# Counting layer 0's softmax sums once per half, with four heads in 32 columns each, and its output projection two steps later

## The chip, the cores and the metric

The kernel runs on one core of one Trainium2 chip. The metric is the device time of one execution in microseconds (us); smaller is better. Before the change the median of three executions is 3203.17 us (3202.34 to 3205.19).

## The reference

There are 16 graphs of 1024 nodes with 256 features (`x`), each with its own 0/1 adjacency matrix. Two attention layers follow each other, layer 0 with 4 heads of 64 columns, layer 1 with 8 heads of 32 columns and biases on q, k and v:

```python
h = maximum(_layernorm(x), 0)
scores = einsum('bhne,bhme->bhnm', Q, K) * scale
attn = softmax(where(adj > 0, scores, -inf), axis=-1)
heads = einsum('bhnm,bhme->bhne', attn, V)
x = x + concat(heads) @ Wo.T + bo
```

The softmax divides by a sum over all 1024 keys. The kernel leaves that division to the end: it multiplies the exponentials by V first and divides the 64 (or 32) columns of a head by the sum of its exponentials afterwards. The change is about how these sums are counted and brought to where they divide.

## The kernel before

**Tiling.** Everything is kept transposed: scores are [128 keys x 512 queries]. A *half* is 512 of a graph's 1024 queries. A *group* is the heads that fill the 128 partitions of one output tile: two heads in layer 0, four in layer 1; so a half has two groups, g = 0 and 1. A group is walked in *steps* of four score blocks of 128 x 512: four steps for a layer 0 group (two heads by two blocks of keys), eight for a layer 1 group (four heads, one block of keys). Graph b has 16 steps in layer 0 and 32 in layer 1.

**One step.** `scores` issues four matmuls (L447) into two pairs of PSUM banks. `exponentials` masks each pair on VectorE (L463, out of PSUM into the step's tile p) and exponentiates it on ScalarE (L469). Two steps later `weigh` multiplies p by V into the group's accumulator po (L481). `Stream.run` writes the order out: at an even step on which a large matmul job is due (a projection `k`, `q`, `values` or `end_half`), the weighing is put off to the next step, which then weighs two steps' tiles. So a "large" even step is followed by an odd step with a double weighing.

**Order of the steps.** After graph 0's layer 0, layer 0 of graph b+1 and layer 1 of graph b alternate. In what follows, a *period* is these 48 steps: steps 0 to 15 are layer 0 of graph b+1 (the code's `a` is step 0), steps 16 to 47 are layer 1 of graph b (the code's `c` is step 16). There are 15 periods, and 32 steps of the last layer 1 after them. `later(i, f)` hangs a job on step i; within a step, jobs stand behind the masking of that step's two pairs, large ones last.

**The buffers that matter.** All score pairs, projections and outputs share three pairs of PSUM banks (`psum_pair`, L115), taken in turn: each new pair waits until the one three before it has been read. The tile p has seven buffers for even steps and two for odd ones (L459), so the mask of an odd step waits until the odd tile of four steps before is no longer read.

**The sums before.** In layer 0, `add_tiles` (L486) adds a group's sixteen exponential blocks on VectorE (L490, L493) and GpSimd (L493, L494, L496) to one tile of [128 keys x 2 heads x 512 queries]. Four steps after the group's last weighing, `count_added` (L348) sums it over the keys on TensorE: per head one matmul with 64 columns of ones (L343), which leaves the sum in all 64 partitions of the head in the PSUM tile pz. In layer 1 GpSimd adds the odd step's tile to the even step's (L582, 128 x 2048 elements) and DMAs with addition (L568) join two such sums; TensorE counts four heads of 32 columns in one go.

Then the chain of a group: `spread` copies pz to the tile s on ScalarE (L362) and spreads one row per head over the partitions by DMA (L375); `invert` takes the reciprocal on VectorE (L383) and writes it to DRAM (L385); `fetch` reads it back broadcast to the head's partitions, into the tile inv (L393); `normalize` multiplies the group's half of `cat` by it on GpSimd (L399); `end_half` multiplies `cat` by Wo (L429, 16 records on TensorE) and adds the result to x (L434). `end_group` (L611) sets their steps. For layer 0 they come 4, 6, 7, 9 and 11 steps after the group's last weighing. In a period the four groups of layer 0 are counted at steps 9, 13, 17 and 21, normalized at steps 14, 18, 22 and 26, and the two halves are projected at steps 20 and 28. `block_inputs(mine, 1, ...)` at L766 puts the q projection of layer 1's second half on step 22.

s and inv have one buffer each. The reciprocals' DRAM tiles have four buffers for each layer.

Of the kernel before, what the change touches and what calls it, by code (L numbers as in the profile page):

```python
# [10 lines left out]
F32 = mybir.dt.float32  # L11
# [7 lines left out]
P = 128  # L19
# [69 lines left out]
def fast_program(ctx, tc, a, w, loads, chk):  # L89
# [3 lines left out]
    nc = tc.nc  # L93
    x, adj, out = a["x"], a["adj"], a["out"]
    B, N, E = x.shape
# [216 lines left out]
    class Group:  # L312


        def __init__(self, inp, mask, qh, g, half):
            self.inp, self.mask, self.qh, self.g, self.half = inp, mask, qh, g, half
            self.layer = inp.layer
            self.D = E // HEADS[self.layer]
            self.per = P // self.D
            self.scale = 1.0 / math.sqrt(self.D)  # L320
            self.n = f"{inp.n}_{qh}_{g}"
            self.n_f = self.per * 512 // P
            self.last = qh == QH - 1 and g == 1

            self.hurry = False

            self.waits = ((6, 6), (7, 7), (8, 6), None)[2 * qh + g]

            self.brief, self.pairs = self.last and inp.b == B - 2, False
# [8 lines left out]
        def count(self, p, start, stop):  # L338

            if start:  # L340
                self.s = ps_o.tile([P, 512], F32, tag="pz", name=f"pz_{self.n}")
            for r in range(self.per):
                nc.tensor.matmul(  # L343
                    self.s[r * self.D : (r + 1) * self.D, :], w.ones.to_broadcast([P, self.D]), p[:, r, :],
                    start=start, stop=stop,
                )

        def count_added(self):  # L348
            self.count(self.t, True, True)

        def copy_out(self):
            if self.g == 0:
# [5 lines left out]

        def spread(self):

            s = work.tile([P, 512], F32, tag="s", bufs=1, name=f"s_{self.n}")
            nc.scalar.copy(tiled(s), by_tile(self.s))  # L362
            inp, k = self.inp, 2 * self.qh + self.g
            if k == 0:

                pool, tag = small, f"sums{self.layer}"
                if self.layer and inp.b == B - 1:
                    pool, tag = adjp, "adj"
                inp.sums = pool.tile(
                    [P, 4 * self.n_f], F32, tag=tag, bufs=1, name=f"sums_{inp.n}"  # L370
                )
            self.sn = inp.sums[:, ts(k, self.n_f)]
            lanes = P // self.per
            for r in range(self.per):
                nc.sync.dma_start(  # L375
                    self.sn[r * lanes : (r + 1) * lanes, :],
                    s[r * self.D : r * self.D + 1, :].rearrange("r (c f) -> r c f", f=self.n_f),
                )

        def invert(self):  # L380

            vn = small.tile([P, self.n_f], F32, tag="vn", bufs=1, name=f"vn_{self.n}")
            nc.vector.reciprocal(vn, self.sn)  # L383
            vd = dram.tile([self.per, 512], F32, tag=f"vd{self.layer}", name=f"vd_{self.n}")
            nc.sync.dma_start(self.lanes(vd), vn)  # L385
            self.vd = vd

        def fetch(self):

            vd = self.vd  # L390
            self.inv = work.tile([P, 512], F32, tag="inv", bufs=1, name=f"inv_{self.n}")
            for r in range(self.per):
                nc.sync.dma_start(  # L393
                    self.inv[r * self.D : (r + 1) * self.D, :], vd[r].partition_broadcast(self.D)
                )

        def normalize(self):
            o = self.half.cat[:, self.g, :]
            nc.gpsimd.tensor_mul(o, o, self.inv)  # L399

        def finish(self):

            inp, qh = self.inp, self.qh
            inv = work.tile([P, 512], F32, tag="inv", bufs=1, name=f"inv_{self.n}")
            py = psum_pair(f"py_{self.n}").rearrange("p a (t e) -> p (a t) e", e=E)
            rows, cat = xs[inp.b, qh], self.half.cat
            dst = quarters(out, inp.b, qh)
            for h in range(2):
                q = ts(h, 256)
                nc.vector.reciprocal(tiled(inv)[:, ts(h, 2)], by_tile(self.s)[:, ts(h, 2)])  # L410
                nc.vector.tensor_mul(cat[:, self.g, q], cat[:, self.g, q], inv[:, q])
                for i in (2 * h, 2 * h + 1):
                    for c in range(2):
                        nc.tensor.matmul(
                            py[:, i, :], cat[:, c, ts(i, P)], w.o[self.layer][:, c, :],
                            start=(c == 0), stop=(c == 1),
                        )
            for h in range(2):
                t = ts(h, 2)
                nc.vector.tensor_add(rows[:, t, :], py[:, t, :], rows[:, t, :])  # L420
                for g in range(4):
                    nc.sync.dma_start(dst[g][:, t, :], rows[ts(g, 32), t, :])
# [84 lines left out]
    class Stream:  # L507
# [103 lines left out]
        def end_group(self, i, gr):  # L611

            if gr.hurry:
                for f in (gr.spread, gr.finish, gr.inp.test):
                    self.later(i, f)
                return

            if gr.layer == 0:
                self.later(i + 4, gr.count_added)
                at = 4, 6, 7, 9, 11  # L620
            else:
                at = ((6, 12, 15, 19), (7, 12, 14, 17, 19), (6, 9, 11, 14), None)[2 * gr.qh + gr.g]
                if gr.pairs:
                    at = 2, 5, 6, 7, 9
                elif gr.last:
                    at = 4, 6, 7, 9, 11
            for k, f in zip(at, (gr.spread, gr.invert, gr.fetch, gr.normalize)):
                self.later(i + k, f)
            if gr.last:

                k = 7 if gr.layer or gr.inp.b == 0 else 37
                self.later(i + k if gr.inp.b + gr.layer < B - 1 else len(self.steps) + 2, gr.inp.test)
            if gr.g == 1:
                self.later(i + at[4], gr.end_half)
# [119 lines left out]
    for b in range(B - 1):  # L754
        mine, a, c = inputs[1][b], first[b + 1], second[b]
        if b == 0:

            norms(mine, 0, a + 5, a + 6, a + 8, a + 9, whole=True)
            half_inputs(mine, 0, a + 11, a + 12, a + 14, a + 14)
            norms(mine, 1, a + 13, a + 14, a + 15, c, whole=True)  # L760
            half_inputs(mine, 1, c + 1, c + 3, c + 6, c + 4)
        else:
            norms(mine, 0, a - 20, a - 16, a - 15, a - 14, bias=a)
            block_inputs(mine, 0, a - 10, a - 8, a - 4, a, a + 2, a + 8)
            norms(mine, 1, a - 14, a - 10, a - 8, a - 6, bias=a + 6)
            block_inputs(mine, 1, a, a + 6, a + 7, c, c + 6, c + 2)  # L766
        for i, u in zip((0, 2, 4, 6, 8, 10, 12, 13), range(NT)):
            later(a + i, masks[b].second, u)
        if b + 2 < B:
# [275 lines left out]
```

## Time and profile before

| what | before |
|---|---|
| median of three executions | 3203.17 us |
| the profiled execution, its own time | 3201.31 us |
| its span, first to last instruction | 3199.5 us |
| granted TensorE clock, mean | 0.997 |
| VectorE busy | 2532.5 us, 79% |
| GpSimd busy | 2352.4 us, 74% |
| ScalarE busy | 2242.4 us, 70% |
| layer 0's counting matmuls (L343, 64 columns), 256 records | 66.5 us |
| layer 1's counting matmuls (L343, 32 columns), 992 records | 129.5 us |
| copies of pz (L362), 128 | 72.9 us |
| normalizing multiplications (L399), 127 | 185.4 us |
| layer 0's reciprocals (L383, 128 x 8), 64 | 12.0 us |

One fp32 matmul leaves two records in the profile, so layer 0's 256 records are 128 matmuls, two for each of 64 groups. Matmuls on disjoint columns of the array run beside each other, so the time of such a set is read from the start of the first to the start of what follows.

From the start of one step's scores to the next, the profile shows the same pattern in every period from the second on; a period takes between 195.1 and 195.6 us. These are step lengths of the sixth period (layer 0 of graph 6, layer 1 of graph 5), whose step 0 starts 1113.76 us into the span:

| step | 9 | 13 | 17 | 20 | 21 | 22 | 26 | 27 | 28 | 29 | 30 | 31 |
|---|---|---|---|---|---|---|---|---|---|---|---|---|
| us | 6.36 | 6.36 | 5.51 | 4.72 | 3.93 | 4.70 | 2.15 | 3.21 | 4.75 | 2.92 | 2.07 | 3.29 |

The profile's engines are PE (TensorE's matmuls), PEld (its weight loads), DVE (VectorE), ACT (ScalarE), POOL (GpSimd) and SP (the queue that issues most DMAs).

### The profile page before, as it was taken

To read this page: it belongs to the slowest core of one execution; us is meant where nothing else is said; L and a number is where in the kernel's file an instruction comes from. 1 tells how busy PE (TensorE), PEld (TensorE's weight loads), DVE (VectorE), ACT (ScalarE), POOL (GpSimd) and SP (SyncE) were. 2 spreads that over 40 slices of the span, in tenths; PEclk is the share of its full clock that TensorE was granted. 3 is DMA by queue.
4 is the path that set the end of the run, shared out by engine and by line. 5 is a ranking of instruction groups with operands and counts; after the bars stand their busy time and mean duration, and the time that the engine had idled before them with its cause. 6 is when DMAs were issued, how large, how long until landed. Compare 5 with 4: busy or idle time off the path is not lost.

```text
span 3199.5 us, 44432 instructions
## 1 busy us (share of the span) xinstructions
PE 3153.7 (99%) x16662; PEld 1212.4 (38%) x16662; DVE 2532.5 (79%) x2786; ACT 2242.4 (70%) x2472; POOL 2352.4 (74%) x1103
## 2 busy tenths in 40 slices
PE   8999999999999999999999999999999999999998
PEld 3443433433334333333433334343343333333332
DVE  5677787887878888787887878878788887887776
ACT  5667677776767767677676776767777676775765
POOL 4567677786877868678686776877778687786776
PEclk9999999999999999999999999999999999999999
DMA  6326556364563645646465463655636456462321
GB/s 132 53 47 131 108 112 130 88 135 106 111 134 92 130 104 109 131 99 129 95 127 117 101 134 92 131 104 112 135 88 133 108 111 135 91 131 62 85 62 32
DMA packets 347792, 341.21 MB, mean 107 GB/s; under 512 B 196016, under 2 KB 290480, under 8 KB 330544
## 3 DMA queue, kind: packets, MB, share of 16 engines
q0 software_dynamic: 37584, 173.03, 29.2%
q1 hardware_dynamic: 309984, 165.26, 21.5%
q8 instruction: 133, 2.18, 0.3%
q14 instruction: 91, 0.75, 0.1%
HBM read 149.95 MB, written 47.96 MB: 62 GB/s over the span
## 4 chain that ended last, share of the span: by engine, by line
PE 89%; ACT 4%; DVE 3%; POOL 2%; issue 1%; DMA 1%; SPq 0%; DVEq 0%; POOLq 0%; ACTq 0%
PE ps L447 31%; PE po L481 27%; PE pq L266 13%; PE py L429 7%; PE pv L302 6%; PE pz L343 5%; DVE p L463 2%; ACT p L469 2%; ACT hn L210 1%; ACT mask L163 1%; POOL p L582 1%; POOL rstd L199 0%; ACT v L306 0%; DVE st L191 0%; DMA hT<-turned 0%
## 5 line engine op out<-in xcount | busy, mean ns | idle before, releaser
L463 DVE SCALAR_TENSOR_TENSOR p<-mask,ps 128x1024 f32<-128x1024 fp8e5 x1536 | 1796.8, 1212 | 461.3 <-PE ps L447 423.6
L469 ACT ACTIVATE p<-p 128x1024 f32<-128x1024 f32 x1536 | 1609.4, 1056 | 784.9 <-DVE p L463 745.4
L582 POOL TENSOR_TENSOR p<-p,p 128x2048 f32<-128x2048 f32 x255 | 1171.3, 4596 | 250.0 <-PE po L481 152.3
L447 PE MATMUL ps<-qT,kT 32*128 32x512 f32 (+1 forms) x6144 | 1134.1, 631 | 7.2 <-ACT v L306 4.4
L481 PE MATMUL po<-p,v 128*32 128x512 f32 (+1 forms) x6144 | 990.6, 601 | 2.1 <-ACT cat L354 1.8
L447 PEld LDWEIGHTS ps<-qT,kT 32*128 32x128 f32 (+1 forms) x6144 | 363.7, 184 | 706.2 <-issue 308.6
L494 POOL TENSOR_TENSOR p<-p 128x1024 f32<-128x1024 f32 x128 | 301.9, 2358 | 284.0 <-DVE p L493 275.3
L481 PEld LDWEIGHTS po<-p,v 128*32 128x32 f32 (+1 forms) x6144 | 229.2, 118 | 690.8 <-issue 500.3
L493 POOL TENSOR_TENSOR p<-p 128x1024 f32<-128x1024 f32 x64 | 150.8, 2357 | 173.3 <-DVE p L490 101.5
L266 PE MATMUL pq<-hT,wk 128*128 128x512 f32 x512 | 242.8, 618 | 8.9 <-DMA hT<-turned 6.3
L302 PE MATMUL pv<-wv,hT 128*128 128x256 f32 x1024 | 237.8, 385 | 0.0
L266 PE MATMUL pq<-hT,wq 128*128 128x512 f32 x512 | 236.6, 605 | 0.0
L429 PE MATMUL py<-wo,cat 128*128 128x256 f32 x1008 | 235.5, 386 | 0.5 <-POOL cat L399 0.2
L302 PEld LDWEIGHTS pv<-wv,hT 128*128 128x128 f32 x1024 | 189.4, 190 | 70.5 <-DVE p L463 30.4
L429 PEld LDWEIGHTS py<-wo,cat 128*128 128x128 f32 x1008 | 185.6, 190 | 72.5 <-issue 31.4
L343 PE MATMUL pz<-p,ones 128*32 128x512 f32 (+1 forms) x1248 | 196.1, 595 | 0.8 <-ACT s L362 0.8
L399 POOL TENSOR_TENSOR cat<-cat,inv 128x512 f32<-128x512 f32 x127 | 185.4, 1460 | 5.0 <-DMA inv<-vd 3.1
L219 POOL TENSOR_TENSOR x<-x,bo 128x1024 f32<-128x1024 f32 x64 | 152.1, 2376 | 15.8 <-DMA bo<-in_bo_dram 15.8
L490 DVE TENSOR_TENSOR p<-p 128x1024 f32<-128x1024 f32 x128 | 163.2, 1275 | 0.0
L210 ACT ACTIVATE hn<-x,shift,rstd 128x256 f32<-128x256 f32 x256 | 138.2, 588 | 24.9 <-DMA turned<-hn 17.7
L496 POOL TENSOR_TENSOR p<-p,p 128x1024 f32<-128x1024 f32 x64 | 151.5, 2367 | 5.0
L266 PEld LDWEIGHTS pq<-hT,wk 128*128 128x128 f32 x512 | 94.4, 194 | 153.3 <-issue 112.9
(51 smaller groups left out, 1665.4 us busy)
## 6 DMA issues: line engine op xcount, KB each, us to landing
p<-p POOLq DMA_DIRECT2D x133, 1024.0 KB, 7.7
adj<-in_adj_dram POOLq DMA_DIRECT2D x128, 256.0 KB, 4.2
turned<-hn SPq DMA_DIRECT2D x58, 512.0 KB, 2.9
hT<-turned SPq DMA_DIRECT2D x232, 128.0 KB, 3.1
x<-in_x_dram SPq DMA_DIRECT2D x128, 128.0 KB, 2.7
inv<-vd SPq DMA_DIRECT2D x128, 128.0 KB, 2.9
inv<-vd SPq DMA_DIRECT2D x252, 64.0 KB, 3.6
out_dram<-x SPq DMA_DIRECT2D x124, 128.0 KB, 2.4
```

Source lines behind the costliest of these rows:

```text
L210: nc.scalar.activation(hn[:, ts(i, E)] if whole else self.blocks(half)[:, :, i, :], rows if whole else rows.rearrange("p (c q) -> p c q", ...
L266: nc.tensor.matmul(pq[:, m, :], wt[self.layer][:, c, ts(m, P)], self.hT[half][:, c, :], start=(c == 0), stop=(c == 1),)
L302: nc.tensor.matmul(pv[:, i, :], self.hT[half][:, c, ts(i, P)], w.v[self.layer][:, c, :], start=(c == 0), stop=(c == 1),)
L343: nc.tensor.matmul(self.s[r * self.D : (r + 1) * self.D, :], w.ones.to_broadcast([P, self.D]), p[:, r, :], start=start, stop=stop,)
L399: nc.gpsimd.tensor_mul(o, o, self.inv)
L429: nc.tensor.matmul(py[:, i, :], self.half.cat[:, c, ts(i, P)], w.o[self.layer][:, c, :], start=(c == 0), stop=(c == 1),)
L447: nc.tensor.matmul(st.ps[i // 2][:, i % 2, :], gr.inp.kT[r * D : (r + 1) * D, gr.g, ts(kt, P)], gr.inp.qT[gr.qh][r * D : (r + 1) * D, gr.g ...
L463: nc.vector.scalar_tensor_tensor(out=half, in0=gr.mask.m[gr.qh][:, kt, :].unsqueeze(1).to_broadcast([P, 2, 512]), scalar=-EDGE if gr.layer ...
L469: nc.scalar.activation(half, half, AF.Exp, scale=gr.scale)
L481: nc.tensor.matmul(gr.o[r * D : (r + 1) * D, :], gr.inp.v[:, kt, h * D : (h + 1) * D], st.p[:, i, :], start=(kt == 0), stop=(kt == NT - 1),)
L494: nc.gpsimd.tensor_add(a, a, b)
L582: nc.gpsimd.tensor_add(one, one, st.p)
```

## The change

Layer 0's sums are counted once for a half. When the first group (g = 0) ends, nothing is scheduled but its summed tile is remembered. At the second group's count, four matmuls with 32 columns of ones each count all four heads, side by side. So there is one copy out of pz, one spread (now four DMAs of one row to 32 partitions), one reciprocal (128 x 16 in place of two of 128 x 8) and one write to DRAM for a half. `fetch` reads two tiles inv, one for each group, and `normalize` does both multiplications one behind the other at the step at which the second group's stood.

s and inv now come from one ring of two buffers (the tag "inv" of the pool `work`), and both layers' reciprocals from one ring of four DRAM tiles.

For graphs 1 to 14 layer 0's `end_half` stands 13 steps behind the last weighing in place of 11: in a period the projections move from steps 20 and 28 to 22 and 30. The q projection of layer 1's second half moves from step 22 to 20 (for periods with the block inputs and graphs below the last). Graph 0's and graph 15's projections stay where they were.

```diff
-            self.n_f = self.per * 512 // P
+            self.n_f = 16
...
-            for r in range(self.per):
+            for r, of in enumerate(p if type(p) is list else [p[:, r, :] for r in range(4)]):
                 nc.tensor.matmul(
-                    self.s[r * self.D : (r + 1) * self.D, :], w.ones.to_broadcast([P, self.D]), p[:, r, :],
-                    start=start, stop=stop,
+                    self.s[ts(r, 32), :], w.ones.to_broadcast([P, 32]), of, start=start, stop=stop
                 )
 
         def count_added(self):
-            self.count(self.t, True, True)
+            both = self.half.first.t, self.t
+            self.count([t[:, r, :] for t in both for r in range(2)], True, True)
...
-            s = work.tile([P, 512], F32, tag="s", bufs=1, name=f"s_{self.n}")
+            s = work.tile([P, 512], F32, tag="inv", name=f"s_{self.n}")
...
-            inp, k = self.inp, 2 * self.qh + self.g
+            inp, k = self.inp, 2 * self.qh + self.g if self.layer else self.qh
...
-            lanes = P // self.per
-            for r in range(self.per):
+            for r in range(4):
                 nc.sync.dma_start(
-                    self.sn[r * lanes : (r + 1) * lanes, :],
-                    s[r * self.D : r * self.D + 1, :].rearrange("r (c f) -> r c f", f=self.n_f),
+                    self.sn[ts(r, 32), :],
+                    s[32 * r : 32 * r + 1, :].rearrange("r (c f) -> r c f", f=self.n_f),
                 )
...
-            vd = dram.tile([self.per, 512], F32, tag=f"vd{self.layer}", name=f"vd_{self.n}")
+            vd = dram.tile([4, 512], F32, tag="vd", name=f"vd_{self.n}")
...
-            self.inv = work.tile([P, 512], F32, tag="inv", bufs=1, name=f"inv_{self.n}")
-            for r in range(self.per):
-                nc.sync.dma_start(
-                    self.inv[r * self.D : (r + 1) * self.D, :], vd[r].partition_broadcast(self.D)
-                )
+            self.inv = {}
+            for g in (self.g,) if self.layer else range(2):
+                inv = self.inv[g] = work.tile([P, 512], F32, tag="inv", name=f"inv_{self.n}_{g}")
+                for r in range(self.per):
+                    nc.sync.dma_start(
+                        inv[ts(r, self.D), :],
+                        self.vd[r if self.layer else 2 * g + r].partition_broadcast(self.D),
+                    )
 
         def normalize(self):
-            o = self.half.cat[:, self.g, :]
-            nc.gpsimd.tensor_mul(o, o, self.inv)
+            for g, inv in self.inv.items():
+                o = self.half.cat[:, g, :]
+                nc.gpsimd.tensor_mul(o, o, inv)
...
             if gr.layer == 0:
+                if gr.g == 0:
+                    gr.half.first = gr
+                    return
                 self.later(i + 4, gr.count_added)
-                at = 4, 6, 7, 9, 11
+                at = 4, 6, 7, 9, 13 if 0 < gr.inp.b < B - 1 else 11
...
-            block_inputs(mine, 1, a, a + 6, a + 7, c, c + 6, c + 2)
+            block_inputs(mine, 1, a, a + 6, a + 7, c, c + (4 if b < B - 2 else 6), c + 2)
```

## The prediction

> **What bounds the kernel now.** I read the busy shares and the chain of waits first, then the sums by stage of one period, then TensorE's timeline, last the other engines' around the moved projection.
>
> ```profile
> PE 3153.7 (99%) x16662; PEld 1212.4 (38%) x16662; DVE 2532.5 (79%) x2786; ACT 2242.4 (70%) x2472; POOL 2352.4 (74%) x1103
> PE 89%; ACT 4%; DVE 3%; POOL 2%; issue 1%; DMA 1%; SPq 0%; DVEq 0%; POOLq 0%; ACTq 0%
> ```
>
> TensorE is busy nearly always and carries most of the chain. A busy matmul may still be one that waits inside, so I go by starts. The sixth period's two stages (layer 0, then layer 1; columns: window, length, then busy time and instructions of each engine):
>
> ```profile
> core 0: us, PE busy (x) PEld busy (x) DVE busy (x) ACT busy (x) POOL busy (x), PEclk, DMA share, GB/s
> 1113.76:1192.89 79.13, 79.13 (x341) 30.97 (x337) 63.99 (x64) 51.06 (x56) 53.28 (x28) 1.00 0.48 106
> 1192.89:1308.90 116.01, 115.67 (x698) 44.01 (x696) 95.05 (x111) 88.17 (x99) 94.45 (x42) 1.00 0.59 119
> ```
>
> In layer 0 the others have slack: VectorE 64 of 79 us, GpSimd 53. In layer 1 VectorE and GpSimd stand at 95 and 94 of 116: little slack, and only as long as TensorE's large jobs, which need neither, are spread evenly.
>
> **What the counting gives.** TensorE's timeline in layer 0 (start, time, instruction); steps 5 and 9 each count one set, the first four heads in 32 columns (layer 1's), the second two in 64:
>
> ```profile
> 1141.62 3.65 PE L481 MATMUL po<-p,v 128*64 128x512 f32 x16
> 1145.20 1.06 PE L343 MATMUL pz<-p,ones 128*32 128x512 f32 x8
> 1146.19 1.99 PE L447 MATMUL ps<-qT,kT 64*128 64x512 f32 x8
> ...
> 1161.25 3.65 PE L481 MATMUL po<-p,v 128*64 128x512 f32 x16
> 1164.73 1.03 PE L343 MATMUL pz<-p,ones 128*64 128x512 f32 x4
> 1165.69 1.99 PE L447 MATMUL ps<-qT,kT 64*128 64x512 f32 x8
> ```
>
> From start to start a set of two takes 1165.69 - 1164.73 = 0.96 us, a set of four 0.99: they do run side by side. But the weighing ahead takes 1145.20 - 1141.62 = 3.58 before the set of four and 3.48 before the set of two. So among 64-column work a set of four costs 0.99 + 0.10 - 0.96 = 0.13 more.
>
> Step 9 and step 17 lose a set (0.96 each, of 64 columns among 64-column work). Step 13 exchanges its set: 0.13 more. Step 21 stands among layer 1's 32-column work, where sets of four take 0.97 (1253.05 - 1252.08 below in the same view): even. That is 1.92 - 0.13 = 1.79 us less TensorE work in each period.
>
> The Trainium skill, "TensorEngine Tiling (Array Packing)", section "Tiling Modes", says that changing the tiling mode drains the array. It speaks against the change at step 13 alone and gives no figure; the 0.13 agrees with it. Left out, it would make the gain 1.92 a period, 2 us more in all.
>
> What else goes (a ScalarE copy of 72.9/128 = 0.57, a reciprocal of 0.19, DMAs) lies beside TensorE's work and is worth nothing here.
>
> **What the move costs.** The end of the second half, steps 25 to 31. Steps start at 1231.73, 1234.66, 1236.81, 1240.02 (28), 1244.77, 1247.69, 1249.76 (31), 1253.05 (32).
>
> ```profile
> 1234.05 4.57 POOL L582 TENSOR_TENSOR p<-p,p 128x2048 f32<-128x2048 f32 x1 [3.07 <-PE po L481]
> 1238.65 2.35 DVE L463 SCALAR_TENSOR_TENSOR p<-mask,ps 128x1024 f32<-128x1024 fp8e5 x2 [0.47 <-POOL p L582]
> 1238.92 0.89 POOL L568 DMA_DIRECT2D p<-p  x1 [0.30 <-POOL p L582]
> 1239.53 1.59 POOL L399 TENSOR_TENSOR cat<-cat,inv 128x512 f32<-128x512 f32 x1
> 1240.78 4.84 POOL L582 TENSOR_TENSOR p<-p,p 128x2048 f32<-128x2048 f32 x1
> 1241.15 3.69 PE L429 MATMUL py<-wo,cat 128*128 128x256 f32 x16
> 1241.19 2.35 DVE L463 SCALAR_TENSOR_TENSOR p<-mask,ps 128x1024 f32<-128x1024 fp8e5 x2 [0.19 <-PE ps L447]
> 1248.87 2.35 DVE L463 SCALAR_TENSOR_TENSOR p<-mask,ps 128x1024 f32<-128x1024 fp8e5 x2 [0.50 <-PE ps L447]
> 1249.76 1.51 PE L447 MATMUL ps<-qT,kT 32*128 32x512 f32 x8
> ```
>
> Two rules are seen. An odd step's mask waits for GpSimd's add of the odd tile four steps before (only two odd buffers): step 27's starts at 1238.65, 0.03 behind the add that ends at 1238.62. And the second pair of scores waits for a free PSUM pair: step 31's scores wait for the first mask of step 30, which ends at 1248.87 + 1.21 = 1250.08, and the weighing follows 1.12 later (1251.20).
>
> Now the projection leaves step 28, and GpSimd gets a second normalization ahead of the add at 1240.78. In the old clock, with steps up to 27 as they are:
>
> - Step 28: scores 1.07, weighing 1.00 (step 30's: 1249.76 - 1248.76). Ends 1242.09 in place of 1244.77. Its masks stay at 1241.19 to 1243.54, then four statistics until 1244.78.
> - Step 29: its second scores wait for step 28's first mask (1242.40); the weighing starts at 1243.51, the step ends at 1244.51.
> - GpSimd: the add ends at 1245.62 before; a normalization more (1.29, its median) makes it 1246.91. Step 29's masks start at 1246.94; the first ends at 1248.15, the second at 1249.29.
> - Step 30: from 1244.51 its second scores wait until 1248.15, so end at 1249.26. The projection, in the pair that step 29's second mask frees, runs from 1249.3 for 3.62. Ends 1252.92.
> - Step 31: scores 1.07, the double weighing 1.85, the count 0.97. Ends 1256.8, against 1253.05: **3.8 us later**.
>
> The projection's own time is only moved; TensorE stands idle in step 30 for 1249.26 - 1244.51 - 1.07 = 3.7 us. The large jobs at 24 and 30 now leave five small steps between them, in which GpSimd needs 4.57 for every two and TensorE only 4.1. Large jobs at 32 and 34 let everything catch up, so I expect nothing further. Bounds: if the added normalization cost nothing, the add ends at 1245.62 and the loss is 2.5; if GpSimd held nobody, the mask would follow the statistics at 1244.78, and 1.6 is lost still. Upward, a normalization of 1.59, as in the row: 4.1. I take 3.8, because step 27's and 31's masks start right at the add's end.
>
> **The other steps.** The spread is four DMAs in place of two. Before layer 1, VectorE waits for them:
>
> ```profile
> 1191.53 1.28 SPq L375 DMA_DIRECT2D sums<-s  x2
> 1194.18 0.20 DVE L383 RECIPROCAL vn<-sums 128x8 f32<-128x8 f32 x1 [0.41 <-DMA sums<-s]
> ```
>
> Two more issues of 0.64 delay this reciprocal by 1.28, and behind it the masks of steps 16 and 17, their sums and the kernel's whole VectorE queue. TensorE's large jobs in 16 and 18 hide most: step 18's masks come behind step 17's two adds, and step 19's second scores would wait about 0.5. Bounds 0 and 1.28; I take 0.3.
>
> At step 18 two normalizations stand ahead of the first layer 1 add: it ends about 1.3 later, and step 21's mask by up to 1; step 22's scores have that much room, so 0. The projection and the q projection change places between 20 and 22; both take some 3.65 of TensorE. The second half's two fetches are issued until 1231.71 now; two more of 0.59 each and the 3.1 to landing make it about 1236, before the normalization at 1239.53. The ring of s and inv: each allocation finds its buffer's normalization or spread past, since s and inv alternate in layer 1; 0. The first group's summed tile is held until step 13 or 21 and its buffer wanted at 16 or 24; 0.
>
> **The sum.** Graphs 1 to 14: 14 x (3.8 + 0.3 - 1.79) = 32.3. Graph 0 keeps its place: -1.79 at most, but it lies in the first period with other waits; -0.9. Graph 15 keeps the projection two steps behind two normalizations: -1.79 and up to 1.29 twice; -0.3. Together +31 on the profiled execution's 3201.3 (span 3199.5, 1.8 around it), that is 3232; the median stands 1.9 above it: **3234 us**.
>
> **The rivals.**
>
> - *Faster: the wait stays covered.* If step 29's mask isn't held (the adds run earlier than I reckon), only counting changes: 15 x 1.79 + 0.9 = 28 less, 3175. For it: TensorE 99% busy, and all such waits on the add come to little now:
>
> ```profile
> DVE p L463 <- POOL p L582: 35.4, 62, 1.2
> ```
>
>   Against: 62 waits show that the adds already end last at odd steps; only the projection at 28 covers step 29's. Chance 0.1.
> - *About no change.* The loss at the lower bound 1.6 to 2.0: 14 x (1.8 - 1.79) - 1.2, so 3202. Needs GpSimd's order not to matter. Chance 0.07.
> - *Slower still: the reciprocal's wait reaches TensorE in full.* 14 x (1.28 - 0.3) = 14 more, 3248. Against: VectorE idles 0.60 before step 18's masks and 2.37 before step 19's (its timeline), which takes up 1.28. Chance 0.1.
> - *Slower, smaller: the loss is near 2.5* because the two normalizations overlap the add: 14 x (2.5 + 0.3 - 1.79) - 1.2 = 13, so 3216. Chance 0.15.
>
> My forecast has the rest, 0.58, with 3225 to 3243 for it. The range takes in the two other slower cases and stops short of no change: 3207 to 3250. No change is within 0.2%, 6.4 us, which is about what measurements here can tell. Faster 0.10, same 0.07, slower 0.83.
>
> **What would show it.** Step 13 0.13 longer, 9 and 17 0.96 shorter. Step 30 some 8.4 us long, with VectorE's masks of step 29 released by the add L582, starting some 4.8 us behind step 29's start; waits of masks on L582 up from 35 to about 80 us. If step 30 takes 4.7, my reading of the odd buffers is wrong, and the kernel is faster. If the loss appears at step 19 too, the spread's DMAs are dearer than I took them.

## The result, and the profile after

| | before | after |
|---|---|---|
| median, us | 3203.28 (3202.34 to 3205.19, 4 runs) | 3310.12 (3309.36 to 3313.82, 4 runs) |
| ratio after/before, 95% interval | | 1.0335 [1.0317, 1.0353] |
| profiled execution, its span, us | 3201.3, 3199.5 | 3310.66, 3308.8 |
| granted TensorE clock, mean | 0.997 | 0.987 |

The kernel is 107 us slower. The forecast was 3234, +31: the direction held, the size was missed by a factor of three, and the time lies 60 us outside the range. In the kernel after, the lines named here stand three further down: L447 is L450, L463 L466, L469 L472, L481 L484, L582 L585, L568 L571, L399 L402, L429 L432.

The busy shares of the profile after, and its chain of work by engine:

```profile
PE 3209.7 (97%) x16662; PEld 1232.4 (37%) x16662; DVE 2568.8 (78%) x2754; ACT 2220.1 (67%) x2440; POOL 2348.8 (71%) x1103
PE 69%; DVE 9%; POOL 9%; ACT 5%; issue 3%; DMA 3%; SPq 1%; ACTq 0%; DVEq 0%; POOLq 0%
```

TensorE has as many records as before (16662), is busy 56 us longer, and yet carries only 69% of the chain in place of 89%. VectorE and GpSimd hold 9% each now, where they held 3% and 2%. The same two stages as before, in the sixth period (window, length, then the engines' busy times, granted clock, DMA share, GB/s):

```profile
core 0: us, PE busy (x) PEld busy (x) DVE busy (x) ACT busy (x) POOL busy (x), PEclk, DMA share, GB/s
1146.05:1225.30 79.25, 78.55 (x340) 30.54 (x337) 64.70 (x63) 50.48 (x55) 52.01 (x27) 1.00 0.46 102
1225.30:1350.98 125.68, 122.44 (x699) 46.47 (x697) 97.14 (x110) 87.42 (x99) 95.71 (x43) 0.97 0.54 113
```

Layer 0 keeps its length (79.25 for 79.13), layer 1 takes 9.7 us more at a clock of 0.97 in place of 1.00. Taken apart by step, from the start of one step's scores to the next, as a mean over the third to the fourteenth period (after less before, us):

| step | 9 | 12 | 13 | 17 | 21 | 22 | 24 | 25 | 28 | 29 | 30 | 31 | period |
|---|---|---|---|---|---|---|---|---|---|---|---|---|---|
| us | -0.86 | +0.84 | +0.14 | -0.67 | -0.04 | +1.27 | +0.68 | +1.25 | -2.68 | -0.49 | +8.73 | +0.49 | +8.66 |

The periods sum to 108 of the span's 109. So there are four losses: at step 30, at 22, at 24 and 25, and at 12.

**Step 30.** The timeline of the end of the second half, after (start, time, instruction; in brackets the idle time ahead and what ended it; here and below, rows of other instructions between these are left out). Step 29 starts at 1277.51, step 30 at 1279.95, step 31 at 1291.24:

```profile
1276.19 1.58 POOL L402 TENSOR_TENSOR cat<-cat,inv 128x512 f32<-128x512 f32 x1
1277.44 4.82 POOL L585 TENSOR_TENSOR p<-p,p 128x2048 f32<-128x2048 f32 x1
1279.95 1.13 PE L450 MATMUL ps<-qT,kT 32*128 32x512 f32 x4
1282.29 4.62 DVE L466 SCALAR_TENSOR_TENSOR p<-mask,ps 128x1024 f32<-128x1024 fp8e5 x4 [2.09 <-POOL p L585]
1283.57 2.08 PE L450 MATMUL ps<-qT,kT 32*128 32x512 f32 x4 [2.49 <-DVE p L466]
1285.57 5.74 PE L432 MATMUL py<-wo,cat 128*128 128x256 f32 x16
```

The odd buffer's wait is there as drawn: add, mask (1282.29, 4.78 behind step 29's start), then the second scores. But these scores then take 2.08 for 1.13, and the projection 5.74 for the 3.7 of before. The windows view of the same place says why:

```profile
1282.87:1289.69 6.82, 6.12 (x14) 3.81 (x15) 4.04 (x4) 4.23 (x4) 5.35 (x2) 0.50 0.57 96
```

For 6.82 us TensorE was granted half its clock. This is a second cost behind the wait, which the prediction doesn't have.

**Step 22.** It should start its second scores at once. The timeline there:

```profile
1246.16 4.53 POOL L585 TENSOR_TENSOR p<-p,p 128x2048 f32<-128x2048 f32 x1
1248.33 2.39 DVE L195 TENSOR_TENSOR ve<-mv,numbers 128x4 f32<-128x4 f32 x1
1250.72 1.40 DVE L278 TENSOR_SCALAR qT<-pq,bq 128x512 f32<-128x512 f32 x2
1252.04 1.20 DVE L466 SCALAR_TENSOR_TENSOR p<-mask,ps 128x1024 f32<-128x1024 fp8e5 x1
1252.17 1.13 PE L450 MATMUL ps<-qT,kT 32*128 32x512 f32 x4
```

Before, the sixth period's rows at that place were these (step 20 starts at 1210.75, step 21 at 1215.47, step 22 at 1219.40):

```profile
1210.33 4.55 POOL L582 TENSOR_TENSOR p<-p,p 128x2048 f32<-128x2048 f32 x1
1215.54 0.16 DVE L195 TENSOR_TENSOR ve<-mv,numbers 128x4 f32<-128x4 f32 x1
```

L195 adds eps to four variances per partition. Before, it took 0.16 us there; now 2.39, and it ends at 1250.72, 0.03 behind the end of GpSimd's add (1246.16 + 4.53 = 1250.69). VectorE's queue stands behind it, step 21's mask with it, and step 22's second scores wait for that mask. The Trainium skill, "SBUF — State Buffer", section "SBUF: two separate sides", has the reason: VectorE and GpSimd share a pair of ports under an exclusive lock, and a VectorE operation with two SBUF inputs blocks for the whole of a GpSimd operation that reads SBUF. The trace agrees: mv and eps both lie in SBUF, and the end times meet within 0.03 us; L191 and L192 just ahead, with one input in SBUF, run inside the same add in their usual 0.42 and 0.18 us.

The add gets into L195's way because it is late: as a mean of the twelve periods it starts 2.58 us behind step 20's start, where before it started 0.18 ahead of it. Of these 2.76 us the second normalization makes 1.2. The other 1.5 stand ahead of it: GpSimd's last adds of layer 0 wait for an add of VectorE, and that comes later (1.11 behind step 18's start in place of 0.42 ahead), for the greater part because VectorE waits longer for the first half's reciprocal: 1.50 us a period in place of 0.63.

**Steps 24 and 25.** The timeline around the second half's spread:

```profile
1256.92 0.94 POOL L571 DMA_DIRECT2D p<-p  x1 [0.30 <-POOL p L585]
1256.94 3.34 SPq L375 DMA_DIRECT2D sums<-s  x4
1261.65 1.24 DVE L236 STREAM_TRANSPOSE hn<-hn 128x1024 f32<-128x1024 f32 x1
1264.66 0.25 DVE L383 RECIPROCAL vn<-sums 128x16 f32<-128x16 f32 x1 [1.77 <-DMA sums<-s]
1264.83 2.28 DVE L466 SCALAR_TENSOR_TENSOR p<-mask,ps 128x1024 f32<-128x1024 fp8e5 x2
```

The four small transfers are issued just behind GpSimd's adding DMA of a whole tile, and land late. The issue-to-landing times of the tile s there:

```profile
DMA to landing us min/median/max: 1.7/5.8/6.2
```

Before, GpSimd's adding DMA came behind the two spreads, and both landed within 1.8 us:

```profile
1221.74 1.13 SPq L375 DMA_DIRECT2D sums<-s  x2
1222.64 0.94 POOL L568 DMA_DIRECT2D p<-p  x1 [0.30 <-POOL p L582]
```

The reciprocal is on time in VectorE's queue and waits 1.77 us, with the masks behind it. Over the twelve periods the second half's spreads take 5.9 us to landing as a median, in place of 1.7, and the reciprocal waits 2.17 as a mean, in place of nothing.

**Step 12** gives back what step 9 won:

```profile
1203.39 2.36 POOL L219 TENSOR_TENSOR x<-x,bo 128x1024 f32<-128x1024 f32 x1
1205.71 2.25 POOL L402 TENSOR_TENSOR cat<-cat,inv 128x512 f32<-128x512 f32 x1
1206.61 0.70 PE L432 MATMUL py<-wo,cat 128*128 128x256 f32 x2
1208.01 3.29 PE L432 MATMUL py<-wo,cat 128*128 128x256 f32 x14 [0.70 <-POOL cat L402]
```

TensorE comes 0.86 us earlier to layer 1's projection. GpSimd's bias addition L219 and the normalization behind it are no earlier (counted from step 9's start, the normalization begins at 14.09 now and at 14.11 before), and the projection waits for them.

Two lines of the waits after (total, times, longest), where before had 35.4 and 7.5:

```profile
DVE p L466 <- POOL p L585: 56.1, 61, 2.1
DVE vn L383 <- DMA sums<-s: 46.7, 26, 3.0
```

### The profile page after: what moved, and what is told of

Its sections match the earlier page's. It is cut to its first block, busy times and chain, and to the rows that moved or that the text cites. A ratio compares the mean times of both kernels' runs of the same rounds, so it can differ in the third digit from the quotient of the medians.

```text
span 3308.8 us, 44304 instructions
## 1 busy us (share of the span) xinstructions
PE 3209.7 (97%) x16662; PEld 1232.4 (37%) x16662; DVE 2568.8 (78%) x2754; ACT 2220.1 (67%) x2440; POOL 2348.8 (71%) x1103
## 4 chain that ended last, share of the span: by engine, by line
PE 69%; DVE 9%; POOL 9%; ACT 5%; issue 3%; DMA 3%; SPq 1%; ACTq 0%; DVEq 0%; POOLq 0%
PE ps L450 24%; PE po L484 21%; PE pq L266 10%; PE py L432 6%; DVE p L466 5%; PE pv L302 5%; POOL p L585 4%; PE pz L343 3%; POOL cat L402 2%; ACT p L472 2%; DMA sums<-s 2%; ACT hn L210 1%; SPq L375 1%; POOL p L497 1%; POOL x L219 1%
## 5 line engine op out<-in xcount | busy, mean ns | idle before, releaser
L472 ACT ACTIVATE p<-p 128x1024 f32<-128x1024 f32 x1536 | 1607.5, 1056 | 926.5 <-DVE p L466 892.8
L466 DVE SCALAR_TENSOR_TENSOR p<-mask,ps 128x1024 f32<-128x1024 fp8e5 x1536 | 1794.5, 1213 | 435.4 <-PE ps L450 377.5
L585 POOL TENSOR_TENSOR p<-p,p 128x2048 f32<-128x2048 f32 x255 | 1169.6, 4589 | 324.1 <-PE po L484 225.7
L450 PE MATMUL ps<-qT,kT 32*128 32x512 f32 (+1 forms) x6144 | 1189.8, 634 | 50.6 <-DVE p L466 43.1
L484 PE MATMUL po<-p,v 128*32 128x512 f32 (+1 forms) x6144 | 992.1, 602 | 2.4 <-ACT cat L354 2.4
L450 PEld LDWEIGHTS ps<-qT,kT 32*128 32x128 f32 (+1 forms) x6144 | 377.5, 184 | 788.2 <-issue 305.1
L484 PEld LDWEIGHTS po<-p,v 128*32 128x32 f32 (+1 forms) x6144 | 229.3, 118 | 690.9 <-issue 490.1
L432 PE MATMUL py<-wo,cat 128*128 128x256 f32 x1008 | 261.6, 415 | 12.0 <-POOL cat L402 10.4
L432 PEld LDWEIGHTS py<-wo,cat 128*128 128x128 f32 x1008 | 203.0, 207 | 99.8 <-issue 49.3
L402 POOL TENSOR_TENSOR cat<-cat,inv 128x512 f32<-128x512 f32 x127 | 178.3, 1448 | 5.5 <-DMA inv<-vd 3.4
L437 DVE TENSOR_TENSOR x<-py,x 128x1024 f32<-128x1024 f32 x63 | 77.0, 1222 | 127.7 <-PE py L432 127.7
L493 DVE TENSOR_TENSOR p<-p 128x1024 f32<-128x1024 f32 x128 | 173.7, 1357 | 0.0
L219 POOL TENSOR_TENSOR x<-x,bo 128x1024 f32<-128x1024 f32 x64 | 152.7, 2387 | 16.0 <-DMA bo<-in_bo_dram 15.6
L343 PE MATMUL pz<-p,ones 128*32 128x512 f32 x1248 | 163.2, 595 | 0.8 <-ACT s L362 0.8
```

The lines of the kernel that those rows point to most:

```text
L219: nc.gpsimd.tensor_add(rows, rows, w.bo[self.layer].unsqueeze(1).to_broadcast([P, 4, E]))
L343: nc.tensor.matmul(self.s[ts(r, 32), :], w.ones.to_broadcast([P, 32]), of, start=start, stop=stop)
L402: nc.gpsimd.tensor_mul(o, o, inv)
L432: nc.tensor.matmul(py[:, i, :], self.half.cat[:, c, ts(i, P)], w.o[self.layer][:, c, :], start=(c == 0), stop=(c == 1),)
L450: nc.tensor.matmul(st.ps[i // 2][:, i % 2, :], gr.inp.kT[r * D : (r + 1) * D, gr.g, ts(kt, P)], gr.inp.qT[gr.qh][r * D : (r + 1) * D, gr.g ...
L466: nc.vector.scalar_tensor_tensor(out=half, in0=gr.mask.m[gr.qh][:, kt, :].unsqueeze(1).to_broadcast([P, 2, 512]), scalar=-EDGE if gr.layer ...
```

## The experiments

Each kernel's time is compared with the kernel before on the same chip (medians 3200.8 for e1 to e4, 3202.9 for e5 to e8, 3201.5 for e9 to e12). Step changes are means over the same twelve periods. e1 to e6 and e9 were executed once each, the others four to ten times.

**e1: the two moves alone**, on the kernel before.

```diff
-                at = 4, 6, 7, 9, 11
+                at = 4, 6, 7, 9, 13 if 0 < gr.inp.b < B - 1 else 11
-            block_inputs(mine, 1, a, a + 6, a + 7, c, c + 6, c + 2)
+            block_inputs(mine, 1, a, a + 6, a + 7, c, c + (4 if b < B - 2 else 6), c + 2)
```

> The kernel before with only the steps moved (projections of layer 0 at 22 and 30, q at 20); counting as before, one normalization ahead of each add. If the odd buffers are what stalls step 30 (the add of steps 24 and 25 ends when it did, at 1245.62 of the old clock, and no projection covers step 29's mask), step 30 loses about 2.5 us a period and the kernel takes about 3238; if TensorE's clock halves behind that wait as it does in the changed kernel, up to 2.8 more a period, about 3275. If the second normalization is what stalls it, nothing is lost here and the time stays within 10 us of 3203. Steps 22, 24 and 25 stay as before in either case.

Measured: 3243.27. Only steps 28 to 31 change: -2.68, -0.49, +5.70, +0.49. In nine of the twelve periods the four come to +2.4 to 2.6; in the rest to 4.0 or 5.7. Step 30 in the sixth and in the ninth period, by windows:

```profile
1258.31:1265.58 7.27, 5.87 (x28) 3.55 (x25) 4.84 (x6) 4.34 (x5) 6.97 (x4) 1.00 0.52 88
1852.16:1862.59 10.43, 9.17 (x28) 5.45 (x24) 4.84 (x6) 4.34 (x5) 7.05 (x4) 0.67 0.61 114
```

The other engines' work is the same in both to 0.1 us; the clock is 1.00 in one and 0.67 in the other, and 3.16 us lie between. So the odd buffer's wait costs 2.5 a period without the second normalization, and the clock up to 3.2 on top, in some periods.

**e2: the counting alone**, both moves undone in the kernel after.

```diff
-                at = 4, 6, 7, 9, 13 if 0 < gr.inp.b < B - 1 else 11
+                at = 4, 6, 7, 9, 11
-            block_inputs(mine, 1, a, a + 6, a + 7, c, c + (4 if b < B - 2 else 6), c + 2)
+            block_inputs(mine, 1, a, a + 6, a + 7, c, c + 6, c + 2)
```

> The changed kernel with the projections back at 20 and 28 and q at 22; the sums still counted once. If the move makes the loss at steps 28 to 31 (6 us a period), it goes, but the projection at 28 waits up to 1.3 for the second normalization, and the losses of steps 12, 22, 24 and 25 (0.9, 1.3, 0.6, 1.1) stay: 3203 + 14 x (0.86 - 0.86 - 0.86 + 0.14 + 3.0 + 1.3) = about 3250, no half clock. If all losses came from the move, only the counting's gain is left: 3175 to 3195.

Measured: 3237.85. The counting by itself is 37 us slower, where the prediction gave its matmuls a gain of 28 and took off 4 for the first half's reciprocal. Steps 9, 12, 13, 24 and 25 change as in the kernel after; 22 does not (the q projection is back in it), but 20 loses 1.15 and 28 0.76, both steps with a projection. The projection waits there for the second normalization; step 28 of the sixth period:

```profile
1253.88 0.70 PE L432 MATMUL py<-wo,cat 128*128 128x256 f32 x2
1255.11 3.29 PE L432 MATMUL py<-wo,cat 128*128 128x256 f32 x14 [0.53 <-POOL cat L402]
```

At step 20 it waits 0.37 for the first and 0.52 for the second. The clock stays at 0.997. e1's +42 and e2's +37 come to 80, not 107: the second normalization and the move meet in steps 28 to 31, which lose 6.05 together and 3.02 and 0.76 apart.

**e3: layer 0's first normalization on VectorE**, so that the add behind the pair is not later.

```diff
-                nc.gpsimd.tensor_mul(o, o, inv)
+                (nc.gpsimd if g or self.layer else nc.vector).tensor_mul(o, o, inv)
```

> The changed kernel with the first group's normalization on VectorE in place of GpSimd, so that one stands ahead of each add as before. If the second normalization costs what it delays the adds by, step 29's mask starts 1.3 earlier, step 30 is 1.3 shorter (up to 4 if the clock no longer halves), and step 22's 1.3 goes: 3310 - 14 x 2.6 = about 3274, down to 3235 without half clocks. If the second normalization is hidden and only the move counts, within 10 us of 3310.

Measured: 3276.83. Step 22 loses 0.33 in place of 1.27, steps 28 to 31 together 3.9 in place of 6.05; 24 and 25 stay at +2.07. So the second normalization on GpSimd accounts for most of step 22's loss and for some 2 us of that at steps 28 to 31. What is left there lies near e1's 3.02, where one normalization stands ahead of the add too.

**e4: the two small statistics operations on GpSimd**, L195 and L197, in the kernel after.

```diff
-                nc.vector.tensor_add(ve, mv[:, :, 1], w.eps)
+                nc.gpsimd.tensor_add(ve, mv[:, :, 1], w.eps)
-                nc.vector.tensor_mul(less, mv[:, :, 0], w.minus)
+                nc.gpsimd.tensor_mul(less, mv[:, :, 0], w.minus)
```

> The changed kernel with the two 128 x 4 operations of the layer norm's statistics (lines 195 and 197) on GpSimd, where the power that reads them runs anyway. If step 22's loss of 1.27 us is VectorE held at line 195 by GpSimd's add (2.39 us in place of 0.16), step 22 goes back to 4.7 and the kernel to about 3310 - 14 x 1.27 = 3292. If step 22 loses by the q projection's two copies standing where one add to x stood, it stays, and the time with it (within 6 us).

Measured: 3267.25, some 25 us better than expected. Step 22's loss is gone, and all that left VectorE's queue are the two small operations. Not all of it need be the port at this one place, for the add starts earlier too, 1.79 behind step 20's start in place of 2.58. But in e5, below, it starts at 1.70 with L195 still on VectorE, and step 22 loses 0.49. Steps 24 and 25 fall from +1.93 to +0.41 as well: with step 22 on time, the spread is issued ahead of L571, and three of its four transfers land in 1.7 us. Steps 28 to 31 stay at +6.12. In the sixth period, where the clock happens to hold, step 30 reads:

```profile
1259.51:1267.99 8.48, 5.88 (x29) 3.56 (x25) 4.83 (x6) 4.35 (x5) 8.18 (x4) 1.00 0.40 71
```

8.48 us at full clock, where the prediction wrote "some 8.4 us"; in periods at half clock it takes 9.6 to 11.7.

**e5: the reciprocal one step later** for layer 0, and the fetch with it.

```diff
-                at = 4, 6, 7, 9, 13 if 0 < gr.inp.b < B - 1 else 11
+                at = 4, 7, 8, 9, 13 if 0 < gr.inp.b < B - 1 else 11
```

> The changed kernel with invert and fetch of layer 0 one step later (7 and 8 in place of 6 and 7). If steps 24 and 25 lose 1.9 us a period because VectorE stands at the reciprocal waiting for the four spreading DMAs, that goes: 3310 - 14 x 1.9 = about 3284. If they lose it because all of VectorE is late from step 22 on (line 195), most of it stays and the time is within 10 us of 3310.

Measured: 3278.57. Steps 24 and 25 lose nothing now, so the reciprocal's wait was their cause. Step 22's loss falls to 0.49, which I hadn't expected. The trace gives the reason: the first half's reciprocal no longer waits either, VectorE's add behind it comes 0.9 earlier, GpSimd's adds with it, and L195 is held for 1.46 us in place of 2.39. The second half's spreads still take 5.9 us to landing (median), but nobody waits for them: the reciprocal's wait there falls from 2.17 to 0.16. Steps 28 to 31 lose 6.58, with TensorE at half clock for 6.8 us in 13 of the 15 periods.

**e6: layer 1's bias addition one step later**, on e2.

```diff
-                norms(other, 1, c, c + 4, c + 5, c + 6, bias=c + 42)
+                norms(other, 1, c, c + 4, c + 5, c + 6, bias=c + 43)
```

> The changed kernel with the projections back (as e2, 3238), and GpSimd's addition of the bias to x (line 219, 2.4 us) one step later, so that it stands behind layer 1's last normalization of a period and not ahead of it. If step 12 gives back what step 9 saved because the projection there waits for that normalization, step 12's 0.84 goes: 3238 - 12 = about 3226. If step 12 is slower for another cause (the tiling mode, the weights), it stays at 3238.

Measured: 3217.74. Step 12 goes from +0.84 to -0.16: the bias ahead of the normalization in GpSimd's queue was what it waited for. Step 20's loss falls from 1.15 to 0.45. Steps 24, 25 and 28 remain.

**e7: all the mendings at once**: the counting without the moves, counted and brought one or two steps earlier, with e4's and e6's edits.

```diff
-                self.later(i + 4, gr.count_added)
-                at = 4, 6, 7, 9, 13 if 0 < gr.inp.b < B - 1 else 11
+                self.later(i + 3, gr.count_added)
+                at = 3, 5, 6, 7, 11
```

> The sums counted once for a half as in the change, but one step earlier (count and spread 3 steps behind the last weighing, invert 5, fetch 6, both normalizations 7, where GpSimd waits for TensorE anyway; projections back at 11, q at 22), the statistics' two small operations on GpSimd and the bias one step later. If the counting is worth what the steps 9, 13, 17 and 21 show (about 1.75 us a period) and all losses were collisions of its chain with GpSimd's adds, VectorE's queue and the projections, this takes 3203 - 28 = about 3175. If two normalizations and four DMAs cost by themselves wherever they stand, it stays above 3203.

Measured: 3212.35, ratio 1.0032 [1.0019, 1.0044]: a miss by 37 us. Steps 22, 24 and 25 are clean; step 28 loses 2.02 and step 19 0.94 (the +0.84 at step 12 and +1.00 at step 20 are counting sets moved there). The second half's `fetch` now meets the adding DMA that `spread` met before (L571 is issued at 1223.37, the first fetch at 1224.31). Timeline:

```profile
1232.61 2.53 POOL L402 TENSOR_TENSOR cat<-cat,inv 128x512 f32<-128x512 f32 x2 [1.94 <-DMA inv<-vd]
1235.10 4.58 POOL L585 TENSOR_TENSOR p<-p,p 128x2048 f32<-128x2048 f32 x1
1239.71 4.61 DVE L466 SCALAR_TENSOR_TENSOR p<-mask,ps 128x1024 f32<-128x1024 fp8e5 x4 [1.83 <-POOL p L585]
```

The landing times of the tile inv there:

```profile
DMA to landing us min/median/max: 5.8/7.2/7.8
```

A late fetch holds the normalizations, they hold the add, the add holds an odd mask: the odd buffer's wait once more, set off by a transfer.

**e8: e4's and e6's edits on the kernel before**, to see what they are worth without the counting.

> The kernel before with only the two side edits of e7: the statistics' two small operations on GpSimd and the bias one step later. The time per step of the kernel before has no stall at steps 12 or 20 to 25, so I expect 3190 to 3205; a clear gain here would have to be taken off the gain of e7.

Measured: 3197.16, ratio 0.9982 [0.9973, 0.9992]. By steps: -0.16 at step 12, -1.35 in graph 0's layer 0, little else.

**e9: three odd buffers and six even ones**, in the kernel after.

```diff
-        st.p = pp.tile([P, 4, 512], F32, tag=f"p{odd}", bufs=2 if odd else 7, name=f"p_{st.n}")
+        st.p = pp.tile([P, 4, 512], F32, tag=f"p{odd}", bufs=3 if odd else 6, name=f"p_{st.n}")
```

(The two tiles of these tags that stage the first adjacencies follow.)

> The changed kernel with three buffers for the tiles of odd steps and six for those of even steps (two and seven before). If step 29's mask waits at GpSimd's add because there are two odd buffers, it now starts behind the statistics, step 30's wait falls below what halves TensorE's clock (about 0.6 to 1.6 us left in place of 3.8), and no half clock follows: step 30 loses 1 to 2 instead of 8.7 a period and the kernel takes 3310 - 14 x 7 = about 3215. If step 30 waits for something else, it stays at 3310.

Measured: 3249.72. Steps 28 to 31 lose 1.53 in place of 6.05. Step 30 in the sixth period, by windows, and step 29's masks in the timeline:

```profile
1259.60:1265.87 6.27, 5.87 (x28) 3.55 (x24) 4.83 (x6) 4.35 (x5) 6.27 (x3) 1.00 0.39 65
```

```profile
1257.09 4.83 POOL L585 TENSOR_TENSOR p<-p,p 128x2048 f32<-128x2048 f32 x1
1259.77 2.33 DVE L466 SCALAR_TENSOR_TENSOR p<-mask,ps 128x1024 f32<-128x1024 fp8e5 x2
1262.19 4.83 POOL L585 TENSOR_TENSOR p<-p,p 128x2048 f32<-128x2048 f32 x1
```

The masks start in the middle of the add and wait for nothing, and step 30 keeps the full clock. The 4.5 us that go are the odd buffer's wait and what the clock made of it. The time is 35 us above what I expected, because steps 12, 22, 24 and 25 stay at +0.84, +1.24, +0.64 and +1.46: I had put too much of the whole on step 30.

**e10: three odd buffers in the kernel before.**

> The kernel before with the same buffers. It waits for the odd buffers 35 us in 62 places, nearly all covered: 3195 to 3203; more than 3210 if six even buffers are too few.

Measured: 3198.48, ratio 0.9991 [0.9982, 1.0001]: about nothing, since before no odd wait reaches TensorE.

**e11: e7 with the reciprocal and the fetch one step earlier still**, and layer 1's other bias addition later.

```diff
-                at = 3, 5, 6, 7, 11
+                at = 3, 4, 5, 7, 11
-                norms(other, 0, a + 10, a + 12, a + 13, a + 15)
+                norms(other, 0, a + 10, a + 12, a + 13, a + 15, bias=c + 36)
```

> As e7, with invert and fetch one step earlier again (4 and 5), so that the reciprocals' DMAs are issued ahead of GpSimd's 1 MB adding DMA of step 22 and not behind it, and GpSimd's bias addition of layer 0's first half out of the way of the normalizations at steps 16 and 17. If the DMAs queue behind the 1 MB transfer (7.8 us to landing in e7, 2.9 elsewhere) and so hold the normalizations, step 28's loss of 2.0 goes, and step 19's 0.9 with the bias moved: 3212 - 14 x 2.9 = about 3172. If step 28 loses by the normalizations' own time, it stays above 3195.

Measured: 3173.76, ratio 0.9912 [0.9895, 0.9928]. Busy shares:

```profile
PE 3130.9 (99%) x16662; PEld 1201.4 (38%) x16662; DVE 2490.4 (78%) x2626; ACT 2219.6 (70%) x2440; POOL 2361.3 (74%) x1231
```

The landing times of the tile inv at the second half:

```profile
DMA to landing us min/median/max: 3.1/3.4/7.8
```

In the sixth period two of the four fetches are issued ahead of the adding DMA, at 1208.74 and 1209.28 against 1209.99, and three land within 3.5 us; the fourth, issued 0.57 behind it, still takes 7.8. The normalizations start 3.9 behind step 24's start in place of e7's 5.9, step 28 loses nothing, and what is left is the counting: sets taken from steps 9, 13, 17 and 21 (-0.86, -0.86, -0.89, -1.01), two put into 12 and 20 (+0.84, which holds e8's -0.16, and +0.99). A period is 1.78 shorter. The kernel has the shared ring of s and inv too, so the ring costs nothing that shows.

**e12: e11 with e9's buffers.**

> e11 and the three odd buffers together. If both do what they should, as e11 or a few us below: 3160 to 3172; a loss against e11 would mean that the first group's summed tile is held too long for six even buffers.

Measured: 3167.38, ratio 0.9898 [0.9882, 0.9915]; a period is 2.05 shorter. TensorE is busy 3122.1 of 3163.5 us. It is the best version of the study, and 143 us below the kernel after.

The losses side by side (us a period):

| kernel | 12 | 22 | 24 and 25 | 28 to 31 | whole period | time |
|---|---|---|---|---|---|---|
| after | +0.84 | +1.27 | +1.93 | +6.05 | +8.66 | 3310.1 |
| e1 moves alone | 0 | 0 | 0 | +3.02 | +3.04 | 3243.3 |
| e2 counting alone | +0.84 | 0 | +2.06 | +0.76 | +3.29 | 3237.9 |
| e3 one normalization away | +0.83 | +0.33 | +2.07 | +3.93 | +5.58 | 3276.8 |
| e4 no port conflict at L195 | +0.86 | 0 | +0.41 | +6.12 | +5.64 | 3267.3 |
| e5 reciprocal later | +0.84 | +0.49 | 0 | +6.58 | +6.11 | 3278.6 |
| e9 three odd buffers | +0.84 | +1.24 | +2.10 | +1.53 | +4.30 | 3249.7 |
| e11 chain earlier, no moves | +0.84* | 0 | 0 | 0 | -1.78 | 3173.8 |

\* A counting set that was moved there, not a wait.

## Why the prediction was right or wrong

**The counting, 1.79 a period: right.** Steps 9 and 13 give -0.86 and +0.14, step 17 -0.86 in most periods, step 21 -0.15 where nothing else delays it (as in e2): together 1.73. In the kernel after itself the four come to 1.44, since step 17 is disturbed in two periods and step 21 in most. The set of two was worth 0.86 rather than 0.96, since with it gone the weighing ahead pays the 0.10 that goes with a change of kind; the 0.13 at step 13 was right to 0.01. e11 against e8 (-1.78 and -0.20) gives 1.58 with the sets at other steps.

**The move, 3.8 a period: the mechanism right, its size too small.** The term "step 30" came out as drawn: mask 4.78 behind step 29's start (4.8 said), 8.48 us long in a period at full clock (e4; 8.4 said), 3.73 for the four steps by that step 30 (-2.68 - 0.49 + 8.48 - 2.07 + 0.49). Its bounds held too: 2.5 without the second normalization (e1), 1.6 with nobody held (e9, 1.53). Measured were 6.05. The missing 2.3 is the half clock that follows the wait: the prediction let the scores and the projection behind it run at 1.07 and 3.62. The chain of that step thus costs idle time once as idle time, and once more in the work after it.

**"Step 22's scores have that much room, so 0": failed, +1.27.** The prediction had the add about 1.3 later; it is 2.76 later, because the first half's reciprocal, priced by itself at step 19, delays the same chain and the two delays add up. And the step missed that the add doesn't only delay the mask that needs its buffer: it holds VectorE's L195, which needs nothing of it but the port, and the copies of q (L278, 1.40 us) and the mask come behind L195. e4 takes L195 away and the loss is 0; e3 and e5 each make the add 0.9 to 1.0 earlier, and 0.33 and 0.49 are left.

**"Two more of 0.59 each", the second half's transfers at no cost: failed, +1.93.** The prediction counted issue times on SP's queue, 1.28 at most, and looked at the first half's reciprocal (step 19, +0.3; no loss is seen there, it comes out at step 22). It did not ask what else is on the DMA engines when the second half's spread starts. Behind GpSimd's 1 MB, landing takes 5.8 us for 1.7. e5 shows the cause by the wait, e4 and e11 by the order of issue.

**Step 12: not in the sum, +0.84.** A step that gets shorter moves TensorE up to a projection whose input another engine makes. The prediction asked this of the moved projection and not of step 9's gain. e6 shows it.

The sum over a period: predicted +2.3; clock +2.3, steps 24 and 25 +1.9, step 22 +1.3, step 12 +0.8 more, the gain 0.35 smaller (step 17 by two disturbed periods, step 21), step 19 0.3 less, give 8.65 of the measured 8.66. This is for the twelve middle periods. Graph 15's, put at -0.3, came out 3.7 shorter: it takes 198.4 us before, outside the 195.1 to 195.6 that is given for every period, with a wait of 2.17 for the layer norm's transposed output at its step 30 that is not there after. e1 still has that wait (2.27) and e2 doesn't, so it goes with the counting; why was not taken apart, and as far as the prediction goes the gain was luck.

The waits of masks on the add were to rise to about 80 us and stand at 56.1. The count holds VectorE's idle time alone, 2.09 a period here, and VectorE still had statistics to do for the rest of the wait.

**The rivals.** Faster (0.10) was refuted, about no change too. "The reciprocal's wait reaches TensorE in full" had the right engine and tile, but at the first half alone, and a price of 1.28 where the second half's alone cost 1.93. Its condition was looked up on VectorE's idle time around step 18 alone. The faster rival's 3175 is nearly e11's 3173.8, though that kernel has other edits too.

**Open.** What disturbs step 17 in two of the twelve periods was not looked for. How step 22's loss divides between the late add and the port is bounded by e3, e4 and e5, not measured. What the half clock costs by itself can't be removed with the wait left in; it is read from periods of one kernel that differ in it (e1: 7.27 and 10.43).

## What to carry to other kernels

When work is put in front of an operation on a shared resource, list everything that uses the resource while it runs, and not only the consumers of its result: the port between VectorE and GpSimd, the DMA engines behind a large transfer, the buffer ring. A hole in TensorE's work like that of step 30, some 1.8 us in 3.4, can bring the slower clock behind it and is then to be priced with it, not at its length. Delays on one chain are to be added before they are held against its slack: here a normalization and a reciprocal's wait, each priced alone, made the add late together. Where a job's chain of small transfers must pass a large one, put its issue ahead of it, or what waits for it later: e7 and e11, which differ in that by one step (and in one bias addition), are 39 us apart.

## What the runs showed of the hardware

- **A window needn't be idle for the clock to halve.** Half-clock stretches last 3.41 or 6.83 us (one in e3 lasts 10.24). The one in the sixth period follows 3.41 us in which TensorE's matmuls were busy for 1.62 (0.47). Over the kernels after, e1 and e4, 33 of 34 such stretches (those within 30 us of the span's ends left out) follow 3.41 us with a busy share of 0.63 or less, one follows 0.70; other windows of 0.64 and more are followed by full clock, and between 0.50 and 0.63 both occur. But in e3 seven of eleven follow shares of 0.66 and 0.67, and in e9 four of five follow 0.76 to 0.82, so no threshold can be read from these shares, and the share of the records isn't all that decides. The Trainium skill, "TensorE: Matmul & The Clock Gate", section "Part 1: The HAM clock gate (the "warmup" mystery)", has the window of 3413 ns and the half clock, and puts it behind one idle window; the measurement decides, and it says that a window half idle was enough here.
- **Small transfers behind a large one.** Four spreads of one row landed 1.7 us after issue in e11, ahead of GpSimd's 1 MB adding DMA; in the kernel after, issued just behind it, the first still landed in 1.7 and the others took 5.6 to 6.2. The fetches of inv took 5.8 to 7.8 there in e7, and 3.4 as a median in e11.
- **An operation on four numbers a partition can take 2.39 us in place of 0.16**, if it has two inputs in SBUF and GpSimd is in the middle of a 4.5 us add (L195 at step 21, after and before).
